# Seven block products for pairs of tiles in a dense layer, with combined weights streamed through attention B's memory

## The chip, the cores and the metric

One core of one Trainium2 chip runs the whole program: TensorE (PE) for products, VectorE (DVE), ScalarE (ACT) and GpSimd (POOL) for elementwise work, SyncE (SP) for issuing DMAs. The metric is the device time of one execution in microseconds, median of the runs shown; lower is better.

## What is computed

Two sequences (B = 2) of 1024 tokens with 1024 features, all in float32, so 16 tiles of 128 tokens. Four residual parts follow each other:

```python
x = x + attn_a(layernorm(x), ...)   # 32 heads, causal, plus an adapter of 10 rows
x = x + ffn(layernorm(x), ...)
x = x + attn_b(layernorm(x), ...)   # 8 heads, no mask
x = x + ffn(layernorm(x), ...)
```

The change is in `ffn`, which is used twice with the same weights:

```python
base_out = jnp.einsum('bsd,od->bso', x, W_base) + b_base          # 1024 x 1024
weights = sparsemax(jnp.einsum('bsd,ed->bse', x, W_router) + b_router)   # 8 experts
h = jnp.einsum('bsd,edr->bser', x, lora_A)                         # rank 16
expert_out = jnp.einsum('bser,bse,ero->bso', h, weights, lora_B)
return base_out + expert_out
```

## The kernel before

**Stages.** Stage A computes attention A for both sequences; `proj_a` multiplies its result by the output weights and adds x; then comes stage B: the first FFN of sequence 0, called f(0,0) here, `project_b` of sequence 0 (the q, k and v of attention B), and attention B. While attention B of sequence 0 runs, the first FFN of sequence 1, its `project_b`, and the second FFN's tiles are worked between its rounds; what is left of the second FFN follows as a tail. A part of the second FFN has four tiles, one of the first has eight.

**What sets the order.** PE's order is that of the program text (a manual schedule), in stage A POOL's too, in stage B SP's too. The order of DVE and ACT is made by a scheduler at build time. Dense work is written as generators that yield the estimated nanoseconds of each step. `Filler.run` takes steps from the generator in front until a round's allowance is spent: FILL_A in attention A, in attention B `FILL_B`, whose first value holds for the first 64 rounds and whose second for the rest. `fill.chore` queues a small DVE step, one of which is taken with each dense step.

**An FFN part (`ffn`, L1167).** The tile is the unit. `fetch` loads x of a tile (512 KB) on SP's queue; `normalize` makes the layer norm (statistics and `xn` on DVE, two small steps on ACT) and adds `b_base` to x on POOL; `transposed` (L273) flips `xn` by TensorE in two halves of four 128x128 blocks, each through a PSUM bank, from which `evac` copies by ACT (L243) and DVE (L241) in turn. Then for each tile: eight products of 136 columns give the LoRA's hidden values and the router's logits together (`hp`); thirteen small DVE steps (L1203 to L1225) make the sparsemax weights and `hw`; sixteen 128x512 products with `wb` give the base layer in two halves of columns (`base`); `hw` is flipped (`ht`), copied by ACT (`hwT`, L1253), and one expert product for each half is added to the same PSUM bank (`experts`); DVE adds the bank to x (L1240). The next tile's transposes stand between these products, so that each tile's normalization has a whole tile of PE work beside it.

**PSUM.** In stage B a pool has three banks under one tag, `ps`, in rotation; `bank` takes the next. `hp`, the base sums, the transposes, and `bv` and `bq` of `project_b` all come from it. Attention B has its own four banks for scores. `block_bank` and `next_bank` hand out banks of the tags in `pair`, in rotation, which `proj_a` uses.

**Seven products.** `proj_a` is already worked in pairs of tiles with the recursion `seven_added` (L1026): for a product of a 2x2 block matrix by another, seven products of sums of blocks in place of eight. Each product is four 128x512 matmuls. `left_factors` (L1067) makes the left sums on DVE. The right ones, `wp["T", 2..4]`, are made once and stay in memory. PE writes products 1, 2, 5 and 3 to one kind of bank and 6, 7 and 4 to the other.

**Memory.** In stage B the tensors `qkb`, `kqb` and `vm` (q, k, v of attention B) have two buffers each, one for each sequence.

Of the kernel before, what the change touches and what calls it, by code (L numbers as in the profile page):

```python
# [20 lines left out]
P = 128  # L21
# [16 lines left out]
FILL_B = 2650.0, 2200.0  # L38
# [109 lines left out]
def tile_model(ctx: ExitStack, tc: tile.TileContext, d, out: bass.AP):  # L148
# [17 lines left out]
    def next_bank(shape, name):  # L166
# [9 lines left out]
    identb = const.tile([P, P], BF16, name="identb")  # L176
    dve.tensor_copy(identb, ident)

    mask = const.tile([P, HF + P], F32, name="mask")
    pool.memset(mask, 0.0)  # L180
    pool.affine_select(
        out=mask[:, HF:], in_=mask[:, HF:], compare_op=ALU.is_ge, fill=NEG,
        base=0, pattern=[[-1, P]], channel_multiplier=1,
    )
    ones = const.tile([P, P], BF16, name="ones")
    pool.memset(ones, 1.0)
# [105 lines left out]
    class Unit:  # L292
# [41 lines left out]
        def s_post(self, piece, p, sc):  # L334
            t, nk, c0, w, o = piece
            last = c0 + w == nk
            m = mask[:, HF + P - w :] if (last and self.causal) else mask[:, :w]
            for i in range(2):
                col = slice(4 * t + 2 * p + i, 4 * t + 2 * p + i + 1)
                if c0 == 0:  # L340
                    self.pr[p, i, t] = self.wk.tile([P, T], F32, tag="pr", name=f"pr_{self.nm}_{p}_{i}_{t}")
                pr = self.pr[p, i, t]

                minimum[0] = dve.tensor_tensor_reduce(  # L344
                    pr[:, c0 : c0 + w], sc[:, i, o : o + w], m, -self.scale, BIG if c0 == 0 else self.part[:, col],
                    ALU.add, ALU.min, (self.nmax if last else self.part)[:, col],
                ).ins
            if last:
                for i in range(2):
                    col = slice(4 * t + 2 * p + i, 4 * t + 2 * p + i + 1)  # L350
                    pr = self.pr.pop((p, i, t))
                    tc.keep_in_program_order(act.activation(  # L352
                        pr[:, :nk], pr[:, :nk], AF.Exp, bias=self.nmax[:, col], scale=-1.0, accum_out=self.sums[:, col]))
# [24 lines left out]
        def shift_rows(self):  # L378
            dt = F32 if self.extra else BF16
            tp = bank([P, 4, P], f"st_{self.nm}")  # L380
            for t in range(4):
# [3 lines left out]
                else:  # L385
                    mm(tp[:, t, :], lhsT=s, rhs=identb, start=True, stop=True)
# [8 lines left out]
        def t_mm(self, piece, h, dst):  # L395
# [4 lines left out]
            if not self.extra:  # L400
                yield w * COL / 4, lambda: pe.matmul(dst[:, o : o + w], lhsT=ones[three, :], rhs=self.rows[three, off : off + w],  # L401
# [156 lines left out]
    def stage_a(wk, big):  # L558
        ca = wk
        cos = ca.tile([P, T], F32, tag="cos", name="cos", bufs=1)  # L560
# [231 lines left out]
        def adapter_keys(g):  # L792
            akp = bank([P, NH], f"akp{g}")
# [4 lines left out]
        def adapter_values(g):  # L798
            avp = bank([NH, 2 * P], f"avp{g}")
# [72 lines left out]
        def project_blocks(b, g):  # L872
# [15 lines left out]
            for r in seven(b, nm, st.pop(("f", b, g)), mul, [P, HF], places, lambda x: rotate(b, g, "k", 0, x), settled):  # L888
# [5 lines left out]
                else:  # L894
                    yield r
                    i += 1
                    if i == 12 and b == 0:
# [21 lines left out]
        def values(b, g):  # L919
# [3 lines left out]
            for r in st["seven", b, e]:  # L923
# [3 lines left out]
                if r is not True:  # L927
                    yield r
                    i += 1
                    if i == 8 and b == 0 and g == e:  # L930
# [80 lines left out]
        def place(kind, i, shape, name):  # L1011
            if kind == "yt" or kind == "x":
                return big.tile(shape, F32, tag={"yt": "t4k", "x": "tt"}[kind], name=name)
            return wk.tile(shape, F32, tag={"s": "sa", "sum": ("sv", "sv", "qr")[i]}[kind], name=name, bufs=2)
# [11 lines left out]
    def seven_added(nm, left, right, ready, sums, x, ended):  # L1026
# [3 lines left out]
        s1, s2, s3 = sums  # L1030

        def product(i, dst, start=True, stop=True):
            ready(i)
            for k in range(4):
                mm(dst, lhsT=left[i][:, k, :], rhs=right[i][:, k, :], start=start and k == 0, stop=stop and k == 3)
                yield HF * COL

        def added(i, s):
            pin_add(x[i], s, x[i])
            ended(i)  # L1040

        first = block_bank([P, HF], f"x_{nm}")
# [4 lines left out]
        pin_add(s2, s1, y)  # L1047
        yield from product(2, first, start=False)
        added(11, first)
# [3 lines left out]
        pin_sub(left[3], left[3], left[6])  # L1053
        z = block_bank([P, HF], f"z_{nm}")
        yield from product(5, z, stop=False)
        pin_add(s3, s1, z)
        added(22, s3)
        y = block_bank([P, HF], f"y4_{nm}", 1)
        yield from product(4, y)
        pin_sub(s1, s1, y)  # L1060
        added(21, s1)
        yield from product(3, z, start=False)
        pin_add(s2, s2, z)
        added(12, s2)
# [10 lines left out]
    def proj_a(b, big, wp, tile_of, then=None, each=None):  # L1075
# [36 lines left out]
        for p in range(NT // 2):  # L1112
# [34 lines left out]
            def ready(i):  # L1147
# [7 lines left out]
                if i == 5:  # L1155
                    if each is not None:
                        each()
                    if then is not None and p == NT // 2 - 1:
                        then.prepare()

            yield from seven_added(nm, left, right, ready, [tile_of("sum", i, [P, HF], f"sum{i}_{nm}") for i in range(3)],
                                   {i: xs[at] for i, at in ends.items()}, lambda i: store(*ends[i]))
# [4 lines left out]
    def ffn(b, k, src, dst, w, wk, tiles, there=lambda t: True):  # L1167
        xs, prepared = {}, {}

        def fetch(t):  # L1170
            xs[t] = wk.tile([P, C], F32, tag="x", name=f"xf{b}_{k}_{t}", bufs=3)
            sp.dma_start(xs[t], src(t))

        def normalize(t):
            nm = f"f{b}_{k}_{t}"
            xn = layernorm(wk, "xn", xs[t], nm, behind=True)
            pool_add(xs[t], xs[t], w["b_base"])
            prepared[t] = (xn, wk.tile([P, NC, P], F32, tag="xt", name=f"xt_{nm}", bufs=2))

        tiles = list(tiles)  # L1180
        fetch(tiles[0])
        fetch(tiles[1])
        yield None
        normalize(tiles[0])
        yield READY
        yield from transposed(*prepared[tiles[0]], f"f{b}_{k}_{tiles[0]}")
        stored = None
        for a, t in enumerate(tiles):
            nm = f"f{b}_{k}_{t}"
            nxt = tiles[a + 1] if a + 1 < len(tiles) else None  # L1190
            if stored is not None:
                sp.dma_start(*stored)
            if nxt is None:
                yield AHEAD
            xnT = prepared.pop(t)[1]
            x = xs.pop(t)
            hp = bank([P, P + NE], f"hp_{nm}")
            for c in range(NC):
                mm(hp, lhsT=xnT[:, c, :], rhs=w["la"][:, c, :], start=(c == 0), stop=(c == NC - 1))
                yield (P + NE) * COL  # L1200
# [5 lines left out]
            prod = small([NE, NE], "prod")  # L1206
# [19 lines left out]
            if nxt is not None:  # L1226
                normalize(nxt)
            ops = {}

            def base(n, c0, c1):  # L1230
                if c0 == 0:
                    ops[n] = bank([P, HF], f"fo_{nm}_{n}")
                for c in range(c0, c1):
                    mm(ops[n], lhsT=xnT[:, c, :], rhs=w["wb"][:, c, n * HF : (n + 1) * HF], start=(c == 0), stop=False)
                    yield HF * COL

            def experts(n):
                cols = slice(n * HF, (n + 1) * HF)
                mm(ops[n], lhsT=hwT, rhs=w["lb"][:, cols], start=False, stop=True)
                dve.tensor_add(x[:, cols], ops[n], x[:, cols])  # L1240
                yield HF * COL

            yield from base(0, 0, NC)
            if a + 2 < len(tiles):
                while not there(tiles[a + 2]):
                    yield WAIT
                fetch(tiles[a + 2])
            elif nxt is None:
                yield AHEAD
            tp = bank([P, P], f"ht_{nm}")  # L1250
            flip(tp, hw.rearrange("p e r -> p (e r)"), ident)
            hwT = small([P], "hwT")
            act.copy(hwT, tp)  # L1253
            yield from base(1, 0, NC // 2)
            halves = [transposed(*prepared[nxt], f"f{b}_{k}_{nxt}", (j,)) for j in range(2)] if nxt is not None else [(), ()]
            yield from halves[0]
            yield from experts(0)
            yield from base(1, NC // 2, NC)
            yield from halves[1]
            yield from experts(1)  # L1260
            stored = dst(t), x
        sp.dma_start(*stored)
# [3 lines left out]
    def project_b(b, w, fk, wk, st):  # L1266
# [15 lines left out]
        qk = st["qk", b] = wk.tile([P, 2, T], F32, tag="qkb", name=f"qk{b}", bufs=2)  # L1282
        kq = st["kq", b] = wk.tile([P, 2, T], F32, tag="kqb", name=f"kq{b}", bufs=2)

        vm = st["vm", b] = wk.tile([P, NT, HB, 2 * EB], F32, tag="vm", name=f"vm{b}", bufs=2)
# [5 lines left out]
        for t in range(NT):  # L1291
# [4 lines left out]
            vp = bank([P, P], f"bv{b}_{t}")  # L1296
# [16 lines left out]
            qp = bank([P, 2, P], f"bq{b}_{t}")  # L1313
# [14 lines left out]
    def project_wo(b, n, yT, w, fk):  # L1328
# [10 lines left out]
        for i in range(4):  # L1339
            t = 4 * n + i  # L1340
            x = xs.pop(i)
            for h in range(2):
# [3 lines left out]
                yield HF * COL  # L1346
# [6 lines left out]
            yield 0.0  # L1353

    def attention_b(w, fk, wk, st, after):
        units, jobs = [], deque()

        def late(r, begun):

            spent = 0.0  # L1360
            if r % 2:
                return spent
            while jobs and spent == 0.0:
                r = next(jobs[0], None)
                while r:
                    spent += r
                    r = next(jobs[0], None)
                if r is None:
                    jobs.popleft()
            return spent  # L1370
# [25 lines left out]
    with tc.manual_schedule(engines={mybir.EngineType.PE}):  # L1396
        with tc.tile_pool(name="big", bufs=2, side="left", reuse_waits="tile") as bigp:
# [35 lines left out]

            def f1(b):
                return ffn(b, 0, lambda t: x1[b, t], lambda t: x2[b, t], w, fk, range(NT))

            def f2(b, tiles):
                return ffn(b, 1, lambda t: x3[b, t], lambda t: out[b, t * P : (t + 1) * P, :], w, fk, tiles,
                           lambda t: ("x3", b, t) in fill.done)

            pj = PoolOf(own.enter_context(tc.tile_pool(name="pj", bufs=2, side="right", reuse_waits="tile")), {"sum": 3, "x": 3, "yt": 1})
# [11 lines left out]
            ps = ctx.enter_context(tc.tile_pool(name="ps", bufs=3, space=bass.MemoryType.PSUM, reuse_waits="tile"))  # L1453
# [9 lines left out]
        wide.append(sh)  # L1463
        fill.add(f1_0)
# [90 lines left out]
```

## Time and profile before

| | us |
|---|---|
| time, median of three runs | 2462.07 (2461.53 to 2462.54) |
| the profiled execution | 2463.84 |
| its span | 2462.1 |
| DVE / ACT / POOL busy | 1389.0 / 1093.6 / 497.1 |
| f(0,0), from 1470 to 1617 | 147 |
| project_b(0), from 1617 to 1676 | 59 |
| attention B with dense work between, from 1676 to 2338 | 662 |
| the tail, from 2356 to 2462 | 106 |

The span is the time from the first to the last instruction of one execution taken by the profiler; the profiled execution has 1.74 us around it. "Busy" is the time in which an engine had work; loading of weights (PEld) lies beside the products. A matmul of float32 has two records, or eight when it is split into columns of 32. In rows of a timeline, the arrow reads out<-in, and a bracket gives the idle time before the row and what ended it. The granted clock of TensorE is a share of its full speed; over the whole span it is 0.996.

### The profile page before, as it was taken

What the parts mean: (1) busy time and instruction counts of PE and PEld (TensorE: products, weight loads), DVE (VectorE), ACT (ScalarE), POOL (GpSimd) and SP (SyncE); (2) the same over time, 40 slices, a digit from 0 to 9 for tenths busy, and PEclk for the clock granted to TensorE, in tenths of its full rate; (3) what the DMA queues carried; (4) which work ended last, traced back from release to release, by engine and by line L of the source; (5) the groups of instructions that cost most, each with busy time, mean ns of one, the idle gap of its engine ahead of it and who ended that gap; (6) DMA issues with size and microseconds to landing.
All of it is one profiled execution on the core that took longest, in us unless ns stands there. A gap on an engine that the chain in (4) does not pass through costs nothing.

```text
span 2462.1 us, 60457 instructions
## 1 busy us (share of the span) xinstructions
PE 2406.4 (98%) x25433; PEld 1091.6 (44%) x25433; DVE 1389.0 (56%) x4199; ACT 1093.6 (44%) x2092; POOL 497.1 (20%) x800
## 2 busy tenths in 40 slices
PE   7999999999999999999999999999999999999999
PEld 4434444455354544445433445584333643333344
DVE  7666665666556666665742343375555865654243
ACT  3346665566565666566642000012354535554200
POOL 1332222222323223222200011101000111111120
PEclk9999999999999999999999999999999999999999
DMA  6633322333233333333212651130101301212121
GB/s 215 211 91 92 92 85 89 96 92 100 92 125 109 94 98 92 96 96 113 83 61 91 210 176 52 43 112 18 46 33 48 126 27 40 82 44 95 37 101 43
DMA packets 142513, 224.35 MB, mean 91 GB/s; under 512 B 12832, under 2 KB 73376, under 8 KB 142240
## 3 DMA queue, kind: packets, MB, share of 16 engines
q1 hardware_dynamic: 142240, 220.48, 27.6%
q8 instruction: 199, 3.26, 0.5%
q14 instruction: 74, 0.61, 0.1%
HBM read 168.01 MB, written 52.43 MB: 90 GB/s over the span
## 4 chain that ended last, share of the span: by engine, by line
PE 87%; DVE 6%; issue 2%; DMA 1%; ACT 1%; POOL 1%; SPq 0%; DVEq 0%; ACTq 0%
PE fo_f L207 11%; PE st L403 9%; PE fo_f L209 7%; PE sc L331 7%; PE y_A L425 5%; PE y L209 5%; PE z L209 3%; PE st L401 3%; PE x L209 3%; PE y_v L209 3%; PE y_B L425 2%; PE y_p L207 2%; DVE pr_A L344 2%; PE bq L207 2%; PE x_v L209 2%
## 5 line engine op out<-in xcount | busy, mean ns | idle before, releaser
L515 ACT ACTIVATE pt<-st 128x1024 f32<-128x1024 f32 (+1 forms) x418 | 425.9, 1019 | 652.0 <-PE st L403 490.7
L352 ACT ACTIVATE pr_A<-pr_A,nmax_A 128x896 f32<-128x896 f32 (+7 forms) x512 | 389.9, 765 | 55.8 <-DVE nmax_A L344 55.0
L344 DVE CUSTOM_DVE_ANT_0 pr_A<-sc,mask 128x512 f32<-128x512 f32 (+3 forms) x512 | 251.1, 537 | 202.1 <-PE st L403 104.1
L331 PE MATMUL sc<-kT,qT 32*128 32x512 f32 (+3 forms) x1536 | 326.4, 521 | 5.1 <-DVE nmax_A L344 2.6
L403 PE MATMUL st<-qT,kT 32*128 32x512 f32 (+3 forms) x1536 | 306.6, 486 | 0.0
L207 PE MATMUL fo_f<-wb,xt_f 128*128 128x512 f32 x558 | 251.3, 593 | 0.4 <-ACT hwT_f L1253 0.4
L344 DVE CUSTOM_DVE_ANT_0 pr_A<-sc,mask,part_A 128x512 f32<-128x512 f32 (+1 forms) x256 | 156.2, 647 | 146.5 <-PE sc L331 97.3
L248 POOL TENSOR_TENSOR xf<-xf,b_base 128x256 f32<-128x256 f32 x128 | 89.3, 729 | 737.6 <-DVE xn_f L270 434.9
L209 PE MATMUL fo_f<-wb,xt_f 128*32 128x512 f32 x1864 | 221.9, 595 | 0.0
L410 POOL TENSOR_SCALAR_AFFINE_SELECT pt<-pt 128x256 f32<-128x256 f32 x256 | 104.9, 427 | 514.4 <-ACT pt L515 514.4
L352 ACT ACTIVATE pr_B<-pr_B,nmax_B 128x1024 f32<-128x1024 f32 x128 | 145.6, 1140 | 41.5 <-DVE nmax_B L344 41.5
L425 PE MATMUL y_A<-pt,v 128*32 128x512 f32 (+3 forms) x1536 | 157.0, 496 | 0.0
L207 PEld LDWEIGHTS fo_f<-wb,xt_f 128*128 128x128 f32 x558 | 102.9, 192 | 112.7 <-issue 112.2
L331 PE MATMUL sc<-kq,qk 32*128 32x512 f32 x512 | 144.3, 640 | 1.3 <-DVE nmax_B L344 1.0
L403 PE MATMUL st<-rows_B,kq 32*128 32x512 f32 x512 | 144.3, 640 | 0.0
L403 PEld LDWEIGHTS st<-qT,kT 32*128 32x128 f32 x1536 | 133.7, 185 | 16.4 <-issue 11.3
L344 DVE CUSTOM_DVE_ANT_0 pr_B<-sc,mask,part_B 128x512 f32<-128x512 f32 x128 | 91.1, 747 | 79.0 <-PE sc L331 78.9
L401 PE MATMUL st<-rows_A,ones 3*128 3x512 bf16 (+3 forms) x768 | 127.7, 329 | 3.8 <-DVE nmax_A L344 3.7
L344 DVE CUSTOM_DVE_ANT_0 pr_B<-sc,mask 128x512 f32<-128x512 f32 x128 | 83.4, 687 | 73.9 <-PE sc L331 73.9
L1240 DVE TENSOR_TENSOR xf<-fo_f,xf 128x512 f32<-128x512 f32 x64 | 44.2, 691 | 139.2 <-PE fo_f L207 113.1
L401 PEld LDWEIGHTS <-ones 3*128 3x128 bf16 x768 | 36.8, 91 | 193.8 <-issue 186.4
L331 PEld LDWEIGHTS sc<-kT,qT 32*128 32x128 f32 x1536 | 113.0, 184 | 20.7 <-issue 7.0
(308 smaller groups left out, 3749.7 us busy)
## 6 DMA issues: line engine op xcount, KB each, us to landing
tt<-td SPq DMA_DIRECT2D x252, 256.0 KB, 2.8
wqk<-in_w_attnT SPq DMA_DIRECT2D x32, 512.0 KB, 5.2
xf<-x SPq DMA_DIRECT2D x32, 512.0 KB, 3.3
xa<-in_x SPq DMA_DIRECT2D x16, 512.0 KB, 5.7
wv<-in_w_attnT SPq DMA_DIRECT2D x8, 1024.0 KB, 5.3
yd<-ys SPq DMA_DIRECT2D x32, 256.0 KB, 2.7
yt<-yd SPq DMA_DIRECT2D x128, 64.0 KB, 2.1
xp<-in_x SPq DMA_DIRECT2D x32, 256.0 KB, 3.4
```

The lines of the kernel that those rows point to most:

```text
L207: return pe.matmul(out, lhsT=lhsT, rhs=rhs, start=start, stop=stop, skip_group_check=True)
L209: pe.matmul(out[i : i + 32], lhsT=lhsT[:, i : i + 32], rhs=rhs, start=start, stop=stop, skip_group_check=True)
L248: pool.tensor_add(dst[:, i : i + 2 * P], a[:, i : i + 2 * P], b[:, i : i + 2 * P])
L331: yield w * COL, lambda: pe.matmul(dst[:, o : o + w], lhsT=self.qt[rows, qc : qc + P], rhs=self.kt[rows, c0 : c0 + w], start=True, stop=True)
L344: minimum[0] = dve.tensor_tensor_reduce(pr[:, c0 : c0 + w], sc[:, i, o : o + w], m, -self.scale, BIG if c0 == 0 else self.part[:, col], AL ...
L352: tc.keep_in_program_order(act.activation(pr[:, :nk], pr[:, :nk], AF.Exp, bias=self.nmax[:, col], scale=-1.0, accum_out=self.sums[:, col]))
L401: yield w * COL / 4, lambda: pe.matmul(dst[:, o : o + w], lhsT=ones[three, :], rhs=self.rows[three, off : off + w], start=True, stop=False)
L403: yield w * COL, lambda: pe.matmul(dst[:, o : o + w], lhsT=self.kt[rows, kb * P : (kb + 1) * P], rhs=rhs, start=self.extra, stop=True)
L410: pool.affine_select(out=dg, in_=dg, compare_op=ALU.is_ge, fill=0.0, base=0, pattern=[[0, 2], [1, P]], channel_multiplier=-1)
L425: pe.matmul(self.y[32 * h : 32 * h + 32, off : off + w], lhsT=self.value(h, kb), rhs=pt[h // 2][:, h % 2, o : o + w], start=self.opens, st ...
L515: act.activation(pt[:, :, low_:wide_], st[:, :, low_:wide_], AF.Exp, scale=ts[0][0].scale)
L1240: dve.tensor_add(x[:, cols], ops[n], x[:, cols])
```

## The change

1. **FFN for pairs of tiles.** `ffn` takes tiles two by two (the odd one first in every list, `seq`). 14 of the 16 pairs do their base product by `seven_added`: 28 matmuls instead of 32 for a pair. The first pair of f(0,0) and the first of f2(0, tiles 0 to 3) stay with eight products (`plain`).
2. **The weights' combinations.** In the first pair of f(0,0) twelve DVE steps make the three combined blocks (T2, T3, T4, of four 256 KB pieces each), and twelve DMAs store them in DRAM (`tf`). Each later pair reads them back, through a ring of four places of 256 KB: when a product has used a place, the piece of the next combination is loaded there. The places are those of `qkb`, `kqb` and `vm` of the sequence whose attention is not running. A fourth combination is made in place in `wb`.
3. **PSUM.** `ps` has one bank; two go to `pair`. `hp` of both tiles of a pair is one bank, of the kind that product 6 takes afterwards; `bv` and `bq` take `next_bank`; transposes and `ht` take the single `ps` bank, `bo` too.
4. **The router** is worked for both tiles after the pair's `hp` (`hidden`), both `hw` are flipped together (`turned`), and the expert products join the base sums: four for a pair, as before.
5. **seven_added** has two sums instead of three: DVE adds three of the x quarters from PSUM, POOL adds sums to x in halves.
6. **Elsewhere.** In stage A the adapter's products take pair banks in place of `ps`, one of them later in the list (step 14 for 12, step 14 for 8). The mask and two constants live in stage A's pool, and a tile of zeros stands for the mask in stage B. `late` gives one output product of attention B to each call. `FILL_B` goes from (2650, 2200) to (2650, 1500). The output is stored in halves of a tile.

The core of the diff, cut:

```diff
-FILL_B = 2650.0, 2200.0
+FILL_B = 2650.0, 1500.0
...
-            akp = bank([P, NH], f"akp{g}")
+            akp = block_bank([P, NH], f"akp{g}") if g else next_bank([P, NH], f"akp{g}")
...
-                    if i == 12 and b == 0:
+                    if i == 14 and b == 0:
...
+        in_halves = in_pieces(pool.tensor_add)
         first = block_bank([P, HF], f"x_{nm}")
         yield from product(1, first, stop=False)
         act.copy(s1, first)
         y = block_bank([P, HF], f"y6_{nm}", 1)
         yield from product(6, y)
         pin_add(s2, s1, y)
+        in_halves(x[12], x[12], s2)
         yield from product(2, first, start=False)
-        added(11, first)
+        ends(11, dve.tensor_add, first)
...
+        def hidden(p):
+
+            hp = block_bank([P, 2, P + NE], f"hp_f{b}_{k}_{seq[2 * p]}", 1)
+            for i in range(2):
+                t = seq[2 * p + i]
+                for c in range(NC):
+                    mm(hp[:, i], lhsT=xts[t][:, c, :], rhs=w["la"][:, c, :], start=(i == c == 0), stop=(c == NC - 1))
+                    yield (P + NE) * COL
+                router(t, hp[:, i])
+
+        def turned(p):
+
+            o, e = seq[2 * p], seq[2 * p + 1]
+            tp = bank([P, 2, P], f"ht_f{b}_{k}_{e}")
+            for i, t in enumerate((e, o)):
+                flip(tp[:, i, :], hws.pop(t).rearrange("p e r -> p (e r)"), ident)
...
+        def combine_weights(slots):
...
+            def make(i, c, op, x, y):
+                t = ts[i, c] = slots[len(ts) % len(slots)]
+                op(t, x, y)
+                sp.dma_start(tf[i, c], t)
+
+            for c in range(4):
+                fill.chore("wb", lambda c=c: make(3, c, pin_sub, b22[:, c], b12[:, c]))
+                fill.chore("wb", lambda c=c: make(2, c, pin_add, ts[3, c], b11[:, c]))
+                fill.chore("wb", lambda c=c: make(4, c, pin_sub, ts[2, c], b21[:, c]))
...
+        yield READY
+        if not late_room:
+            take_room()
+        if behind:
+            fetch(1)
+            yield WAIT
+            yield WAIT
+        normalize(1)
+        yield from turn(0)
+        yield from turn(1)
...
+            turns = {(5, 0): (2, 0), (5, 2): (2, 1), (4, 1): (3, 0), (4, 3): (3, 1)}
+
+            def ready(i):
+                if i == 6:
+                    fill.flush(nm)
+                elif i == 5:
+                    fill.flush("wb1")
+                if not last and i in (6, 7):
+                    normalize(2 * p + 2 + (i == 7))
...
+            def used(i, c):
+                nxt = {2: 3, 5: 4, 3: 2}.get(i)
+                if nxt is not None and not (last and nxt == 2):
+                    piece(nxt, c)
...
-            vp = bank([P, P], f"bv{b}_{t}")
+            vp = next_bank([P, P], f"bv{b}_{t}")
...
-            ps = ctx.enter_context(tc.tile_pool(name="ps", bufs=3, space=bass.MemoryType.PSUM, reuse_waits="tile"))
+            ps = ctx.enter_context(tc.tile_pool(name="ps", bufs=1, space=bass.MemoryType.PSUM, reuse_waits="tile"))
```

## The prediction

> **What bounds the kernel now.** I read the busy times first, then the chain of work that ended last, then stretches of the span, and only then single rows.
>
> ```profile
> PE 2406.4 (98%) x25433; PEld 1091.6 (44%) x25433; DVE 1389.0 (56%) x4199; ACT 1093.6 (44%) x2092; POOL 497.1 (20%) x800
> ...
> PE 87%; DVE 6%; issue 2%; DMA 1%; ACT 1%; POOL 1%; SPq 0%; DVEq 0%; ACTq 0%
> ```
>
> PE is busy for 98% of the span: every matmul less is time less, and every wait that PE does not have today is time more. By stretches (start:end, length, then busy us of PE, PEld, DVE, ACT, POOL, clock, DMA share, GB/s):
>
> ```profile
> 1352.00:1470.00 118.00, 118.00 (x280) 52.31 (x277) 44.06 (x69) 3.33 (x7) 6.65 (x7) 1.00 0.61 200
> 1470.00:1617.00 147.00, 146.66 (x489) 76.30 (x488) 60.08 (x195) 10.05 (x32) 19.56 (x29) 1.00 0.16 56
> 1617.00:1676.00 59.00, 57.14 (x479) 53.84 (x477) 46.26 (x159) 8.51 (x25) 2.84 (x4) 1.00 0.27 90
> ...
> 1984.00:2338.00 354.00, 349.88 (x2846) 115.58 (x2848) 175.82 (x530) 172.21 (x260) 58.97 (x83) 1.00 0.15 55
> ```
>
> They are proj_a, the first FFN part f(0,0), project_b(0), and the second stretch of attention B with FFN work between its rounds. PE is full in all of them; f(0,0) loses 0.34 us in 147. The old order is almost without waits, so the question is how much of the saving the new order returns as waits.
>
> **Removed.** A 128x512 fp32 product costs what proj_a shows:
>
> ```profile
> 1401.14 3.60 PE L207 MATMUL y_p<-wpt,s_p 128*128 128x512 f32 x8
> 1404.57 3.60 PE L207 MATMUL x_p<-wp,yt 128*128 128x512 f32 x8
> ```
>
> Eight records are four products, and the next four start 3.43 us later: 0.858 us each. (Split into columns of 32, where it lies beside attention, it is eight records, and 24 of them took 2.7 us: about the same.) A pair of tiles takes 32 base products now and 28 by the seven; 14 of 16 pairs change, two stay plain. 14 x 4 x 0.858 = **-48.0**. The expert products stay at 64, hp and the flips too.
>
> In stage A the adapter's products leave the bank that the transposes use. PE's waits before them are gone or shorter:
>
> ```profile
> PE st_A L209 <- DVE ae L755: 3.5, 6, 1.5
> ...
> PE akp L207 <- DVE awTA L241: 3.0, 2, 1.5
> PE avp L800 <- DVE ae L755: 2.8, 2, 1.4
> ...
> PE akp L209 <- DVE ae L755: 1.6, 1, 1.6
> ...
> PE akp L207 <- ACT awTA L243: 1.1, 1, 1.1
> ```
>
> The akp and avp rows are 8.5 us. Ends: 0 (the next matmul waits for the same evacuation) and -9; I take **-7**. Of stage B's present waits some 2 us go: **-2**.
>
> **Added on engines that are not the bound.** DVE gets about 95 instructions (left factors, 16 weight combinations), most of 0.6 to 0.7 us; POOL 127 adds of 128x256 at 0.73; SP 212 DMAs, among them 168 loads of 256 KB. In f(0,0) DVE is busy 60 of 147 us, POOL 20, DMA 0.16 to 0.27. A 256 KB `tt` load lands 2.8 us after issue; each ring slot is freed by a product that ends at least 4.5 us before its next reader (another product of 3.43 and what lies beside it), so I cost the stream at nothing; uncovered it would be up to 2.8 us at each of three refills in 14 pairs. The combinations' slots wait for their stores to DRAM (256 KB, 2.8 as for a load), beside the first, plain pair with 27 us of base products. The sums on POOL stand in no path to PE, but for the last store.
>
> **Added on PE's path.** These are waits. I took them from the order of instructions on each engine in the changed program, and durations from the old rows.
>
> (a) *Start of f(0,0).* A pair needs the second tile's normalization at once; before, it had a tile of 18.3 us to hide in. Its chain, statistics to `xn`, takes 4.7 us where project_b starts (last fo_f matmul ends 1616.9, next x transposed 1621.65):
>
> ```profile
> 1621.65 1.06 PE L213 MATMUL xt_b<-ident,xn_b 128*128 128x128 f32 x8 [1.38 <-DVE xn_b L270]
> ```
>
> In the new order four weight subtractions (0.61 each, 2.4) stand on DVE inside this chain: 4.7 + 2.4 = 7.1, less 0.3 of PE work, 6.8. Four half-transposes then share the one "ps" bank, so each waits for the copy of the one before (0.67): 2.0. The common ht and its copy: about 2. **+11**, ends 4 and 14.
>
> (b) *Starts of the other five FFN parts*, minus f(0,0): the same 4.7 chain, part of it beside the transposes of the first tile; then three bank waits of 0.67. 4 each, five of them: **+20**, ends 6 and 27. Attention rounds cover the lower end.
>
> (c) *Product 6 waits for both routers.* hp of both tiles now lies in the bank that product 6 writes, so this waits until both 13-step router chains are through. One chain is 2.58 us:
>
> ```profile
> 1491.78 0.17 DVE L1203 TENSOR_TENSOR z_f<-hp_f,b_router 128x8 f32<-128x8 f32 x1 [1.09 <-PE hp_f L207]
> ...
> 1494.07 0.29 DVE L1225 TENSOR_TENSOR hw_f<-hp_f,z_f 128x128 f32<-128x128 f32 x1
> ```
>
> Alone they end 3.3 us after hp (the first starts 1.85 earlier), just under product 1's 3.43. But the scheduler put the next pair's statistics (two of 0.68, whose tile's DMA must land: 3.3) and an `xn` of 0.81 between them in two of the three seven-product pairs of f(0,0), in two of the four of f2(1), and in shorter form in others. That is 3.5 to 5 us for each such pair, 0.7 to 1.5 for others: 15 in the bare parts and, where attention's minimum passes (0.75 each) stand between but attention matmuls lie beside, 5 more. **+20**, ends 6 and 28. Of all terms this is the one that decides.
>
> (d) *hp's bank* was the previous pair's last product, which DVE must add to x first: 0.75 at each of four bare pair changes, 1 in the rest. **+4**, ends 2 and 6.
>
> (e) *One "ps" bank for transposes* where three rotated, in both project_b's: each tile's second half waits for a copy of 0.67, as far as the bv and bq products don't stand between; in project_b(1) ACT's copies also queue behind exponentials of 1.0 to 1.1. 16 tiles x 0.67 = 10.7: **+10**, ends 3 and 20.
>
> (f) *Less fill per round in attention B's second half* (2200 down to 1500 ns). A round's own matmuls are 1.07 + 0.5, so its length falls from 3.8 to 3.1 us. ACT needs 1.02 + 1.14 in each, DVE two minima of 0.75 and its FFN work: both go from some 58% (100 us from 2100: DVE 58.7, ACT 58.4) to about 72%. The way from sc through minimum and exponential to the next matmul gets 1.5 us of cover where it had 2.2. The moved fill itself is not extra work. **+7**, ends 0 and 20.
>
> **A rule against the trace.** Waits of this length have a second price. After a stretch nearly without matmuls the old profile shows PE at half rate:
>
> ```profile
> 54.00:58.00 4.00, 1.06 (x8) 0.58 (x6) 3.86 (x12) 1.79 (x6) 0.00 (x0) 1.00 0.51 173
> 58.00:60.50 2.50, 2.42 (x12) 1.98 (x12) 2.23 (x5) 0.61 (x2) 0.00 (x0) 0.64 0.02 10
> 60.50:62.00 1.50, 1.50 (x8) 1.37 (x8) 0.29 (x2) 0.58 (x1) 0.00 (x0) 0.50 0.82 333
> ```
>
> The Trainium skill, "TensorE: Matmul & The Clock Gate", Part 1 (The HAM clock gate), says that an idle window of about 3.4 us drops the array to half rate until a busy one of 3.4 us has passed. By the rule each wait above 3.4 us costs 1.7 more: of mine some 8, so +14. By the row it does not follow: a gap of 3.13 us at 620.98 left the clock whole, and the drop above came after 4 us with 1.06 busy in them; the windows run free, so a wait of 4 to 5 us seldom fills one. Only the 6.8 us of (a) is likely to; 1.7 is within its ends. I take 0 and keep +14 for the range.
>
> **Sum.** -48.0 - 7 - 2 = -57. +11 + 20 + 20 + 4 + 10 + 7 = +72. Together +15 on the profiled 2463.84 (span 2462.1 and 1.74 around it): 2479. The shown median, 2462.07, is 1.8 lower, so the forecast is **2477**.
>
> **Rivals.** (1) *Slower, as summed*, 2467 to 2495; chance 0.43. For it: PE is full today, and each new wait is in an instruction order that can be read. (2) *The cover holds.* DVE comes early more often than I assume (it is busy 56%), loads land sooner, and half of the 72 is hidden: -57 + 36 = -21, 2441; chance 0.30. For it: seven products in proj_a run with 118.00 of 118.00 busy. Against it: proj_a has no routers and no statistics between. (3) *Even*, 55 us of waits: 2457 to 2467; 0.10. (4) *Much slower*: the routers' wait and (f) at their upper ends, with the clock's 14: +8 + 13 + 14 on the sum, 2512; 0.17. It decides once DVE is late in every pair. (5) *Nothing is saved*, because a load per quarter of the weights holds PE back: 42 refills of 2.8 are 118 us; the SP queue is nearly empty, so below 0.02, kept inside (4). Rivals 1 and 4 lie above the old time, 2 below.
>
> The bound for no change is 0.2%, 4.9 us. Faster 0.30, same 0.10, slower 0.60. Range 2438 to 2508: its lower end is rival 2 with 3 us more hidden, its upper takes in most of rival 4. The likeliest case's own range is 2467 to 2495.
>
> **What would show it.** PE's busy time near 2358 whatever happens; f(0,0) about 10 us longer than its share, though three pairs save 3.4 each: 147 - 10 + 11 from (a) + 11 of (c) = 159; waits of y6 for hw rows of 3 to 5 us; a start gap of 6 to 7 us in f(0,0); attention B's second half with DVE and ACT above 65%. Wrong if y6 waits under 1 us on average, if part starts cost under 1 us, or if stage A gains nothing.

## The result

The changed kernel takes 2594.51 us (median of four, 2590.59 to 2596.64); the one before, on the same chip, 2462.2. The ratio is 1.0536, with a 95% interval of 1.0518 to 1.0554: slower by 132 us, where I had forecast slower by 15 and a range that ended at 2508. The direction was right; the size was wrong by far. The slower case, rival 4, was put at 2512 and is too small as well.

The busy times of the changed kernel, in the columns of before:

```profile
PE 2403.8 (93%) x25141; PEld 1105.0 (43%) x25141; DVE 1446.3 (56%) x4294; ACT 1100.2 (42%) x2104; POOL 592.5 (23%) x927
```

There are 292 fewer matmul records. Yet PE's busy time has hardly moved (2406.4 to 2403.8), where 48 us less work was to make it 2358.4. And PE is idle for 2588.9 - 2403.8 = 185.1 us, before for 55.7. So the span's +126.8 splits without a rest: -48.0 of work removed, +129.4 of idle time, and +45.4 of busy time for the same work. The clock shows where this last part comes from: the mean granted clock of TensorE is 0.974 and was 0.996. An estimate from these figures: work of 2358.4 us at 0.996 takes 2358.4 x 0.996 / 0.974 = 2412 us, near the 2403.8 measured.

The stretches of the span (start:end, length, busy us of PE, PEld, DVE, ACT, POOL, clock, DMA share, GB/s): the end of stage A up to 1465 (`proj_a`), f(0,0), project_b(0), attention B in three stretches, and the tail.

```profile
1347.00:1465.00 118.00, 118.00 (x281) 52.45 (x278) 34.72 (x56) 3.33 (x7) 26.76 (x37) 1.00 0.61 201
1465.00:1642.00 177.00, 147.05 (x464) 79.06 (x463) 81.34 (x231) 11.71 (x34) 35.96 (x46) 0.92 0.37 119
1642.00:1706.00 64.00, 53.56 (x458) 50.68 (x456) 47.23 (x153) 8.92 (x27) 2.83 (x4) 0.98 0.31 103
1706.00:1935.00 229.00, 206.17 (x1676) 75.01 (x1680) 131.15 (x398) 86.18 (x148) 37.49 (x52) 0.94 0.26 80
1935.00:2045.00 110.00, 99.47 (x1429) 61.20 (x1422) 75.33 (x222) 49.60 (x85) 13.89 (x17) 1.00 0.27 90
2045.00:2394.00 349.00, 308.47 (x2461) 100.17 (x2461) 173.55 (x503) 170.79 (x254) 60.32 (x86) 0.95 0.22 72
2394.00:2589.00 195.00, 161.66 (x500) 85.38 (x498) 78.42 (x222) 12.07 (x34) 49.33 (x68) 0.94 0.38 128
```

f(0,0) takes 177 us where it took 147: 30 us of it idle, and the clock at 0.92. No engine is busy throughout: DVE has work for 81 of 177. That is the picture of a chain in which PE and DVE wait for each other in turn. What PE waits for, from 1460 on (engine, line, awaited, us in total, times, longest):

```profile
PE hp_f L198 <- DVE hw_f L1241: 33.8, 9, 6.8
PE xt_f L204 <- DVE xn_f L261: 21.7, 5, 6.3
PE hp_f L200 <- DVE hw_f L1241: 16.5, 6, 4.1
PE xt_f L204 <- ACT xt_f L234: 14.6, 18, 2.0
PE xt_b L204 <- ACT xt_b L234: 12.0, 15, 2.3
PE xt_f L204 <- DVE mv_f L248: 6.5, 1, 6.5
PE hp_f L198 <- DVE e_f L258: 5.1, 1, 5.1
```

The first and third rows are the surprise. Not product 6 but `hp` itself waits for `hw`: the hidden products of a pair's *second* tile stand still until the router of the *first* tile is through. A timeline of PE in the first pair shows it, with the idle time before a row in brackets:

```profile
1473.16 1.08 PE L204 MATMUL xt_f<-ident,xn_f 128*128 128x128 f32 x4 [6.47 <-DVE mv_f L248]
...
1475.83 3.25 PE L198 MATMUL hp_f<-la,xt_f 128*128 128x136 f32 x16
1485.89 4.00 PE L198 MATMUL hp_f<-la,xt_f 128*128 128x136 f32 x16 [6.81 <-DVE hw_f L1241]
1489.68 8.18 PE L198 MATMUL fo_f<-wb,xt_f 128*128 128x512 f32 x16
```

The same rows in the kernel before, without a wait in front:

```profile
1489.73 2.02 PE L207 MATMUL hp_f<-la,xt_f 128*128 128x136 f32 x16
1491.58 7.03 PE L207 MATMUL fo_f<-wb,xt_f 128*128 128x512 f32 x16
```

A row of sixteen hp records took 2.02 us before; here 4.00. The eight base products behind them (sixteen records) take 8.18 us where they took 7.03. So a wait of 6.81 us costs some 3 us more in the rows behind it. In all, sixteen pairs wait here for 55.4 us (50.3 for `hw`, 5.1 put down to `e`). Where nothing stands inside the router's chain the wait is 2.67, the bare chain; with other DVE steps inside or before it, such as statistics and `xn` of the next pair or attention's minimum, it is 3.4 to 6.8. In two pairs beside attention B it is 0.64.

### The profile page after: what moved, and what is told of

Its sections match the earlier page's. It is cut to its first block, busy times and chain, and to the rows that moved or that the text cites. A ratio compares the mean times of both kernels' runs of the same rounds, so it can differ in the third digit from the quotient of the medians.

```text
span 2588.9 us, 60553 instructions
## 1 busy us (share of the span) xinstructions
PE 2403.8 (93%) x25141; PEld 1105.0 (43%) x25141; DVE 1446.3 (56%) x4294; ACT 1100.2 (42%) x2104; POOL 592.5 (23%) x927
## 4 chain that ended last, share of the span: by engine, by line
PE 84%; DVE 9%; ACT 2%; DMA 2%; issue 1%; POOL 1%; SPq 0%; DVEq 0%; ACTq 0%; POOLq 0%
PE st L394 9%; PE sc L322 7%; PE y_A L416 5%; PE y L200 5%; PE y_f L198 3%; PE z L200 3%; PE st L392 3%; PE z_f L198 3%; PE x L200 3%; PE y_v L200 3%; PE x_f L198 2%; PE y_f L200 2%; PE y_B L416 2%; PE y_p L198 2%; PE hp_f L198 2%; PE x_f L200 2%
## 5 line engine op out<-in xcount | busy, mean ns | idle before, releaser
L239 POOL TENSOR_TENSOR xf<-xf,b_base 128x256 f32<-128x256 f32 x100 | 74.6, 776 | 496.7 <-DVE xn_f L261 452.0
L322 PE MATMUL sc<-kq,qk 32*128 32x512 f32 x512 | 151.1, 667 | 5.1 <-DVE nmax_B L335 5.0
L335 DVE CUSTOM_DVE_ANT_0 pr_B<-sc,zeros 128x512 f32<-128x512 f32 x128 | 83.3, 688 | 85.3 <-PE sc L322 85.3
L335 DVE CUSTOM_DVE_ANT_0 pr_B<-sc,zeros,part_B 128x512 f32<-128x512 f32 x128 | 91.0, 748 | 66.2 <-PE sc L322 66.2
L815 POOL TENSOR_TENSOR qr<-qr,sin 128x256 f32<-128x256 f32 x64 | 60.4, 944 | 225.7 <-DVE qr L811 224.7
L343 ACT ACTIVATION_READ_ACCUMULATOR pr_A<-pr_A,nmax_A 128x1 f32 x512 | 97.2, 190 | 0.0
L200 PE MATMUL y<-tt,wqk 128*32 128x512 f32 x768 | 92.6, 594 | 0.0
L204 PE MATMUL xt_f<-ident,xn_f 128*128 128x128 f32 x256 | 45.1, 305 | 44.0 <-DVE xn_f L261 21.7
```

The source lines that it names most:

```text
L200: pe.matmul(out[i : i + 32], lhsT=lhsT[:, i : i + 32], rhs=rhs, start=start, stop=stop, skip_group_check=True)
L239: pool.tensor_add(dst[:, i : i + 2 * P], a[:, i : i + 2 * P], b[:, i : i + 2 * P])
L322: yield w * COL, lambda: pe.matmul(dst[:, o : o + w], lhsT=self.qt[rows, qc : qc + P], rhs=self.kt[rows, c0 : c0 + w], start=True, stop=True)
L335: minimum[0] = dve.tensor_tensor_reduce(pr[:, c0 : c0 + w], sc[:, i, o : o + w], m, -self.scale, BIG if c0 == 0 else self.part[:, col], AL ...
L343: tc.keep_in_program_order(act.activation(pr[:, :nk], pr[:, :nk], AF.Exp, bias=self.nmax[:, col], scale=-1.0, accum_out=self.sums[:, col]))
L815: pool.tensor_mul(qr[:, hs], qr[:, hs], sin[:, cols][:, hs])
```

## The experiments

All times are medians. Beside the experiments the kernel before took 2463.7 to 2464.8; each ratio is to its runs on the same chip. Since the runs were on several chips, the ratios are the safer comparison between rows; they give the steps below within some 3 us of the differences of medians.

| run | us | ratio to before (95%) | PE busy | PE idle | clock |
|---|---|---|---|---|---|
| changed kernel | 2594.51 | 1.0536 (1.0518 to 1.0554) | 2403.8 | 185.1 | 0.974 |
| e1_routers_last | 2581.43 | 1.0473 (1.0443 to 1.0504) | 2408.7 | 169.5 | 0.974 |
| e2_hp_copied | 2521.72 | 1.0231 (1.0201 to 1.0261) | 2390.1 | 129.5 | 0.982 |
| e4_starts | 2509.97 | 1.0183 (1.0154 to 1.0213) | 2384.4 | 123.5 | 0.985 |
| e5_pb | 2493.35 | 1.0116 (1.0086 to 1.0145) | 2380.4 | 111.1 | 0.987 |
| e6_bank_order | 2481.34 | 1.0072 (1.0049 to 1.0096) | 2376.9 | 102.5 | 0.990 |
| e7_start_banks | 2470.76 | 1.0021 (1.0010 to 1.0033) | 2376.1 | 92.1 | 0.989 |
| e10_ahead | 2462.25 | 0.9993 (0.9984 to 1.0002) | 2376.2 | 89.8 | 0.989 |
| e11_fill_1800 | 2454.13 | 0.9954 (0.9940 to 0.9969) | 2366.4 | 85.9 | 0.991 |
| e12_more_rounds | 2468.72 | 1.0017 (1.0010 to 1.0025) | 2376.0 | 88.4 | 0.991 |
| e8_idle_work | 2588.23 | 1.0501 (1.0460 to 1.0543) | 2431.1 | 158.7 | 0.978 |
| e13b_more_idle_work | 2584.29 | 1.0486 (1.0469 to 1.0504) | 2439.2 | 147.2 | 0.980 |
| e9_adapter_banks | 2464.67 | 0.9999 (0.9991 to 1.0006) | 2411.0 | 55.3 | 0.992 |

Busy, idle and clock are those of the profiled execution. From e2 on, each row down to e11 keeps the edits of the rows above it.

**The hidden products' bank.** First the order alone:

```diff
                     yield (P + NE) * COL
-                router(t, hp[:, i])
+            for i in range(2):
+                router(seq[2 * p + i], hp[:, i])
```

> Edit: both routers' chains stand behind the hidden products of both tiles of a pair; nothing else. Theory A (the second tile's hidden products wait for the first tile's router, because both lie in one bank, and every such wait also costs clock): the rows hp waiting for hw, 50 us in 15 pairs, vanish; product 6 then waits for two chains of 2.67 less 3.43 of product 1, some 2 us in 13 pairs = 26 us. Idle falls by about 25 us and PE's busy time by 15 to 25 through the clock: 2545 to 2560 us. Rival B (DVE is late whatever the order, the wait only changes its name): product 6 waits as long as hp did, time 2580 to 2600.

It gave 13 us, and rival B came nearer than I did. In the waits of this run the hp rows for `hw` are gone, and these stand in their place:

```profile
PE y_f L198 <- issue: 24.7, 7, 6.6
...
PE y_f L200 <- issue: 13.2, 3, 6.0
```

The row names no engine, but a timeline of the second pair does: the second `hw` ends at 1529.20, and product 6 starts at 1529.31, after 4.99 us of idle time. All ten of these waits end 0.1 us after a second `hw`.

```profile
1528.91 0.29 DVE L1241 TENSOR_TENSOR hw_f<-hp_f,z_f 128x128 f32<-128x128 f32 x1
1529.31 6.58 PE L198 MATMUL y_f<-qkb_f,kqb_f 128*128 128x512 f32 x8 [4.99 <-issue]
```

So my step (c) was a real wait; the earlier one had only stood in front of it: both are cases of one bank that holds two tiles' hidden values while a chain of 13 small steps reads them. To test that, e2 takes the reads out of the bank:

```diff
+            hs = wk.tile([P, 4, P], F32, tag="hwT", name=f"hs_f{b}_{k}_{seq[2 * p]}", bufs=1)
+            hs = hs.rearrange("p a c -> p (a c)")[:, : 2 * (P + NE)].rearrange("p (i c) -> p i c", c=P + NE)
+            act.copy(hs, hp)
+            for i in range(2):
+                router(seq[2 * p + i], hs[:, i])
```

> Edit: as e1_routers_last, and ACT copies the hidden products of both tiles to SBUF at once, the routers read the copy, so product 6 gets its bank after one copy of about 0.5 us. Theory A: no waits of hp or product 6 above 1 us; the flips of hw come after product 6 and have 6.9 us of cover for two chains of 5.3: idle falls by about 45 us against the change and the clock gives back 20 to 35: 2510 to 2530 us. Rival B: the wait moves on to the flips, above 2 us in most pairs, time above 2550.

2521.72: theory A holds. One ACT copy for each pair, with both routers behind it, takes 73 us off the changed kernel. The rows of hp and product 6 for a router are gone; of the flips of `hw` behind product 6, two wait, 1.6 us together. Between the two profiles, idle time fell by 55.6 us, close to the 55.4 of the hp rows, and busy time for the same work by 13.7. Whether one bank for each tile's hidden products would do as well was not tried.

**What a wait costs behind itself.** e8 and e13b leave the changed kernel's order and waits as they are, and add matmuls that nobody reads in places where PE stands still: between the two tiles' hidden products and between the first transposes of a part, in f(0,0) and in the second FFN of sequence 1 alone.

```diff
+                jk = ps.tile([P, 2, HF], F32, tag="sc", name=f"jk{b}_{k}_{fill.spent}", bufs=2)
+                for _ in range(n):
+                    mm(jk[:, 0], lhsT=ident, rhs=w["lb"][:, :HF], start=True, stop=True)
```

> Edit: the changed kernel as it is, with matmuls added whose output nobody reads: three of 128x512 (2.57 us) between the hidden products of the two tiles of each pair of f(0,0) and of the second FFN of sequence 1, and at these parts' starts six (f(0,0)) or two each between the first and the second tile's transposes: 32 matmuls, 27 us of added work, all in places where PE waits at least as long. Theory C (a wait also costs what follows it, through the clock): PE stays at full rate and the time falls by 8 to 20 us although nothing but work was added. Rival D (the waits alone cost, the clock is a matter of load over longer times): time unchanged within 4 us, or up to 27 longer.

34 matmuls (29 us of work; I had counted 32), and 6 us less time by the medians: below the 8 I gave theory C, outside D's band. But there are two runs, and the intervals of the two ratios overlap (1.0460 to 1.0543 and 1.0518 to 1.0554), so e8 alone decides nothing. In its first pair a wait of 4.20 us was left and the hp records behind still took 3.56; in the fourth pair nothing was left of the wait, and they took 2.12, where they had taken 3.61. So e13b closes the waits almost wholly:

> Edit: as e8_idle_work, but the added matmuls fill each wait almost wholly: 7, 5, 3 and 3 of 128x512 (0.86 us each) between the hidden products of the four pairs of f(0,0), 6 and 3 in the two parts of the second FFN of sequence 1, and 7, 3 and 3 at these parts' starts; 49 matmuls, 42 us of work nobody reads. In e8 a wait of 4.20 us was left in the first pair and the clock still fell behind it, while it stayed where the wait was closed. Theory C (waits cost what follows them, through the clock): the hidden products of the second tile take 2.1 us in all pairs of these parts where three of them took 3.5 to 4.0, the clock there is 0.99 or more, and the time is 12 to 20 us below the changed kernel's 2594.5. Rival D: as e8 or longer, 2588 to 2610.

42 us of added work, and the kernel is 10 us faster than the changed one (12 by the ratios, whose intervals don't overlap). The first pair's rows now:

```profile
1478.17 2.02 PE L198 MATMUL hp_f<-la,xt_f 128*128 128x136 f32 x16
1480.02 6.17 PE L198 MATMUL 0_820742.400000013_16967<-lb,ident 128*128 128x512 f32 x14
1488.30 2.12 PE L198 MATMUL hp_f<-la,xt_f 128*128 128x136 f32 x16 [2.10 <-DVE hw_f L1241]
```

And the stretches of f(0,0), the middle, and the tail:

```profile
1463.00:1640.00 177.00, 166.51 (x530) 83.15 (x529) 84.84 (x233) 11.62 (x34) 39.72 (x52) 1.00 0.38 122
1640.00:2390.00 750.00, 664.97 (x5970) 285.41 (x5970) 422.03 (x1263) 314.18 (x511) 110.75 (x155) 0.95 0.24 80
2390.00:2586.00 196.00, 181.99 (x594) 88.51 (x588) 83.07 (x232) 13.40 (x38) 52.33 (x73) 1.00 0.40 129
```

The clock is 1.00 in the two edited stretches, 0.92 and 0.94 in the changed kernel, and still 0.95 in the middle, which was not edited. These windows don't begin with the stretches; the gain shows between the first transpose of f(0,0) and the first of project_b(0), in the changed kernel and then in e13b:

```profile
1464.76 0.60 PE L204 MATMUL xt_f<-ident,xn_f 128*128 128x128 f32 x4
1642.33 0.60 PE L204 MATMUL xt_b<-ident,xn_b 128*128 128x128 f32 x4
...
1467.97 0.60 PE L204 MATMUL xt_f<-ident,xn_f 128*128 128x128 f32 x4
1639.59 0.60 PE L204 MATMUL xt_b<-ident,xn_b 128*128 128x128 f32 x4
```

That is 177.6 us and 171.6. The second FFN of sequence 1, from its first transpose to the end, takes 174.3 and 167.9. So the two edited stretches are 12.4 us shorter. In these two executions stage A and the unedited middle are 9.9 us longer, so the profiled times differ by less than the medians. Theory C is right in kind: the clock follows PE's waits, and work in the waits holds it. Its size is at the lower edge of what I had expected (10, not 12 to 20). In the first pair one can see why: the first hidden products take 2.02 us for 3.25, but from the last transpose before them to the second hidden products it is 10.6 us for 11.0, since the DVE chain between ends no sooner. So slow products lie in part beside a chain that PE waits for anyway, and the time that the clock cost in the whole changed kernel is probably below the 45 us of busy time.

**The other waits, one edit at a time.** The second tile's normalization before the part begins:

```diff
         normalize(0)
+        if not behind:
+            normalize(1)
         yield READY
```

> Edit: e2_hp_copied, and the second tile of a part is normalized in the step before the part begins (all parts but one), beside the work of the part before. The waits for xn at the starts were 28 us in six parts, 23 of them in the five that are edited, up to 6.5 each. If they are the second cause and cost clock too: 20 to 35 us less than e2_hp_copied. If DVE has no room earlier, or the start then waits for its other tile: less than 5 us.

11.7 us less: between the two expectations. The starts of f(1,0) and f2(0, tiles 0 to 3) still waited 3 us each, and a new wait of 4.1 us came up (a flip of `hw` behind statistics).

In project_b the second half of each transposition on a bank of the pair:

```diff
-                yield from transposed(*ready[t + 1], f"b{b}_{t + 1}")
+                yield from transposed(*ready[t + 1], f"b{b}_{t + 1}", (0,))
+                yield from transposed(*ready[t + 1], f"b{b}_{t + 1}", (1,), by=next_bank)
```

> Edit: e4_starts, and in project_b the second half of each transposition takes a bank of the pair instead of the single one. The waits for ACT's copy between the halves were 5.4 us in project_b(0) and 6.6 us in project_b(1): 8 to 12 us less than e4_starts if they are real; nothing if the bank of the pair is held by bv or bq just as long.

16.6 us less, more than expected. The rows of xt_b for ACT fell from 12.0 to 1.4 us, and project_b(1)'s last product moved from 2004 to 1988.

No exchange of the pair's banks between pairs of the FFN:

```diff
                                    lambda i: store(*at[i]), ready, also, used)
+            pair.rotate(1)
```

> Edit: e5_pb, and the two kinds of bank are not exchanged at the end of a pair of the FFN, so the hidden products take the bank of product 4, free for two products, and product 1 takes the bank of the last product, whose addition to x then lies beside the hidden products (3.7 us). The waits of hp for the addition to x (rows with L1043) are 9.2 us in e5_pb, two of them 2.2 us long with a slower clock behind: if they go, 9 to 14 us less than e5_pb; if product 1 takes them over, nothing.

12.0 us less, as expected for the first reading: hp's waits for the addition to x went, and product 1 did not take them over.

Alternating banks for the transposes at a part's start:

```diff
-        yield from turn(0)
-        yield from turn(1)
+        for i in range(2):
+            yield from turn(i, (0,), next_bank)
+            yield from turn(i, (1,))
```

> Edit: e6_bank_order, and at the start of each part the transposes alternate between the single bank and the pair's. Waits of xt_f for a copy are 14.6 + 2.4 us in e5_pb, some 12 of them at starts: 6 to 12 us less than e6_bank_order. If the copies themselves (ACT behind exponentials) and not the banks were the limit: below 3.

10.6 us less.

The next part prepared one tile earlier in project_b:

```diff
-            if t >= NT - 2:
+            if t >= NT - 3:
                 yield AHEAD
```

> Edit: e7_start_banks, and project_b prepares the FFN part behind it one tile earlier, so that both its tiles are normalized before their transposes are due. e7 still waits 3.86 us at the start of f(1,0) and 3.80 at that of f2(0, tiles 0 to 3) for xn of the second tile. If these are the starts' cause: 6 to 11 us less than e7 with the clock, about 2461. If the statistics' DMA is late instead: no change.

8.5 us less, and level with the kernel before. The two waits of 3.8 us are gone from its trace.

The allowance of dense work in attention B's second half:

```diff
-FILL_B = 2650.0, 1500.0
+FILL_B = 2650.0, 1800.0
```

> Edit: e10_ahead with FILL_B (2650, 1800) in place of (2650, 1500). My prediction priced the lower allowance at 7 us (0 to 20). If that is right in sign, 1800 is some 3 us faster than e10; if the fill is a matter of where the same work lies, within 1.5 us; if the lower one is the better for this order of work, slower by a few us.

8.1 us less where I expected some 3; the sign of term (f) is right, and its size more than I took. This kernel, 2454.13 us, is 0.46% faster than the one before.

> Edit: e10_ahead, and the part f2(0, tiles 4 to 7) stands back for five rounds of attention instead of two at its start, so that its second tile's x (whose place is freed by a store of the part before) is loaded and normalized before PE needs it: e7 waits 7.83 us there, the longest one left, and runs at a lower clock behind. 5 to 10 us less than e10_ahead if rounds without dense work are as full; no gain if those rounds wait for DVE and ACT instead.

A miss: 6.5 us slower than e10. The long wait fell from 8.73 to 4.02 us in its trace, but the time came back elsewhere. Where stays open: the profiled executions don't show the loss (spans of 2466.0 us for e10, its slowest of twelve, and 2464.4 for e12).

**Stage A alone.** The kernel before, with the adapter's products on the pair's banks and at their new places:

```diff
-            akp = bank([P, NH], f"akp{g}")
+            akp = block_bank([P, NH], f"akp{g}") if g else next_bank([P, NH], f"akp{g}")
```

> Edit: the kernel before, with only the change of the adapter's banks and places in stage A. My prediction took 7 us for this, the stage boundaries of the changed kernel suggest 5: 2455 to 2460. If the gain there came from something else (the mask's place, the pool): 2462 to 2466.

No difference: 0.9999, interval 0.9991 to 1.0006. PE's waits of akp and avp left the list (8.5 us), others came or grew (xt_a for `avs` 2.1, st_A for `ae` 3.5 to 4.6), and the profiled execution begins f(0,0) only 3.2 us earlier (1466.6 for 1469.8). The end time has nothing of it. The last scores of attention B begin at 2250.0 in both traces, and in the tail a wait of PE for `xo` before a flip is 2.20 us where it was 0.92, with slow products behind it (the first two rows are e9's, the last that of the kernel before):

```profile
2357.52 0.47 PE L213 MATMUL ht_f<-ident,hw_f 128*128 128x128 f32 x1 [2.20 <-DVE xo L1345]
2358.35 6.42 PE L207 MATMUL fo_f<-wb,xt_f 128*128 128x512 f32 x8 [0.35 <-ACT hwT_f L1253]
...
2356.94 3.70 PE L207 MATMUL fo_f<-wb,xt_f 128*128 128x512 f32 x8 [0.36 <-ACT hwT_f L1253]
```

The clock from 2338 on is 0.97, and was 1.00. This is one execution, among the slowest of 18; the mean clock of the 18 is 0.992 to 0.997, of the kernel before 0.995 to 0.997. So a lower clock in unchanged code takes back at least a part; no run isolates it.

## Why the prediction was wrong, by its steps

**Removed work** (-48.0) holds as a count: e11, with most of the new waits gone, has 2366.4 us of busy PE at a clock of 0.991; an estimate of 2358.4 x 0.996 / 0.991 is 2370. **Stage A** (-7): the interval of e9 allows 2 at most. I had taken PE's waits at their face value, without asking what would be late next, or what a later wait does to the clock.

**Step (c) failed.** It read the bank's conflict as one between product 6 and the routers, and let the second tile's hidden products run beside the first router ("the first starts 1.85 earlier"). In this build a matmul into a PSUM tile waits for the earlier reads of that tile, though it writes other columns: 15 of 16 pairs wait for `hw`, and in e1, where the reads come later in the program, none does. The prediction did not ask what the second hidden group waits for. So the cover that I counted, product 1 with 3.43 us, lay behind the waiting instruction and covered nothing. The term was 20; the rows show 55.4, and e2 removed 73 us with the clock's part. With this wait gone, the wait that step (c) did describe is 37.9 in e1 (24.7 + 13.2); this is an upper figure for (c), since in e1 the first router, too, starts behind both groups.

**The rule on the clock** I set to 0 and kept 14 for the range. This failed too, and one of its two grounds was a misreading. I had read the gap of 3.13 us at 620.98 in a window that ended at 622 (clock 0.98). The row behind it is slow:

```profile
620.98 0.63 PE L213 MATMUL xt_a<-ident,xn 128*128 128x128 f32 x4 [3.13 <-issue]
621.45 3.15 PE L207 MATMUL kp<-xnT,wqk 128*128 128x512 f32 x4
```

Four such records take 1.88 us elsewhere, and the clock from 622.5 to 624.5 is 0.50. So the old trace spoke for a price. In the changed kernel, from 1460 on, all twelve waits above 3.4 us (the shortest 3.45) have slower rows behind them, and so have some of 2.1 to 2.7. The page of the Trainium skill that the prediction weighs ("TensorE: Matmul & The Clock Gate", Part 1, The HAM clock gate) speaks of an idle window of about 3.4 us; the trace agrees in kind, not in the threshold:

```profile
1571.96 2.12 PE L198 MATMUL hp_f<-la,vm_f 128*128 128x136 f32 x16 [2.67 <-DVE hw_f L1241]
...
1611.01 3.61 PE L198 MATMUL hp_f<-la,xt_f 128*128 128x136 f32 x16 [2.67 <-DVE hw_f L1241]
```

Two waits of one length, one with a drop and one without. The rule was the better guide than 0, but 14 was too small as well: it counted 8 waits at 1.7 us, there were more, and the first pair alone paid 3 us behind one.

**The starts**, (a) and (b), 31: the waits for `xn` are 28.2 (21.7 and 6.5), and most of the 14.6 for ACT's copies belongs to them; somewhat low. **(d)**, 4: 9.2 (the hp rows that wait for L1043), and 12.0 us by e6. **(e)**, 10: 12.0 in the rows, 16.6 by e5. **(f)**, 7: not measured at 2200; 300 ns of it bring 8.1. Its reason, DVE and ACT near 72%, did not come true: in the second stretch (2045 to 2394) they are busy for 50 and 49%. **At nothing** I had the stream of weights: rightly, one wait of 2.0 us in 14 pairs (y_f for `qkb_s`), so rival 5 is out.

As a sum: waits of 72 less 9 that go were to be +63; they are +129. The clock, 0, is +45 of busy time. Rival 2, that half is hidden, had its argument from proj_a; in the FFN the cover of the largest wait was behind the waiting instruction, not beside it.

## What to carry to other kernels

When two groups of products share a PSUM tile and readers of the first stand between them in the program, look whether the second waits for these readers, also where the columns differ; here it did. Copying the values out at once, before a chain of small steps reads them, was worth 73 us. Before a wait is priced by what runs beside it, look whether that cover is queued in front of the waiting instruction or behind it. Price a wait on PE at more than its length, look for slow rows well behind a gap and not only at the next one, and treat removed waits as gains only after the next one in line has been looked at.

## What the runs showed of the hardware

Unread matmuls in PE's waits made the kernel faster (42 us of work, 10 us less time); the granted clock in the two edited stretches was then 1.00. And a small DVE step can be stretched beside POOL's additions: at 1481.45 in the changed kernel and at 1526.51 in e1 the 128x64 product of the router takes about 0.75 us while POOL adds, where all 32 in the kernel before take 0.22.

```profile
1525.77 1.40 POOL L239 TENSOR_TENSOR xf<-xf,b_base 128x256 f32<-128x256 f32 x2
...
1526.51 0.74 DVE L1223 TENSOR_TENSOR prod_f<-zs_f,tri 128x64 f32<-128x64 f32 x1
```

The first of these rows is POOL's and the second DVE's, both of e1; no run separates the two engines, so the cause stays a reading.
